# The first weighted row of each tile written by VectorE straight into the accumulator bank

## The chip, the cores and the metric

The kernel runs on one core of a Trainium2 chip. The metric is the device time of one execution in microseconds (us). All data are 32-bit floats unless said otherwise. The engines are called as in the profile: PE (TensorE, matrix multiplications into the accumulator memory PSUM), PEld (its weight loads), DVE (VectorE), ACT (ScalarE), POOL (GpSimd), SP (SyncE, which only issues transfers here).

## The reference

Four graph attention layers with residual connections on 3327 nodes of 512 features; the 3327 x 3327 adjacency is sparse (about 16 neighbours a node). Cut to what matters, with `h` the normalised input of a layer:

```python
for layer in (0, 1, 2, 3):                     # 8, 4, 1 and 8 heads
    h = relu(layernorm(x))
    v = h @ W                                  # 512 features, split into the heads
    e = leaky_relu(v . a_src[i] + v . a_dst[j], 0.2)
    alpha = softmax of e over the neighbours j of i (layers 0, 1 add the node itself)
    y[i] = sum over j of alpha[i, j] * v[j]    # per head
    x = x + (elu(y) if layer in (1, 2) else y)
```

## The kernel before

**First stage (about the first 312 us).** The adjacency is turned into lists of neighbours. The nodes are sorted by how many neighbours they have and cut into 26 tiles of 128 nodes; tile t needs at most `CAPS[t]` neighbours a node, from 36 (tile 0) down to 11 (tile 25). A list holds the node itself as well.

**The layers.** For a tile, slot k means: of each of the 128 nodes the k-th neighbour. A slot is one row of 512 features on each of 128 partitions. POOL fetches it with an indirect transfer (L834) out of a table in device memory that holds the projected features of all nodes; slot 0, the nodes themselves, comes with a plain transfer by SP from layer 1 on (L865). Slots are worked on in groups of up to four; one group is one step. (In layer 0 the first group has three, and the node itself is the last of them; in the other layers it is slot 0.) In a step `scored` (L870 to L895) makes the softmax weights: DVE adds and bends the scores (L887, L889), ACT takes the exponential into the tile `pw` in PSUM (L890). Then `group` (L897 to L921) multiplies and adds:

```python
            m = pools["m"].tile([P, GROUP, F], F32, name="m")
            for q in range(n):
                ...   # DVE: m[:, q, :] = row q of the group times the weights of its heads  (L916)
            for q in range(n):
                nc.tensor.matmul(self.po, ident, m[:, q, :], start=(k0 + q == 0), stop=(k0 + q == K - 1))
```

So DVE writes each weighted row to SBUF (the tile `m`, three buffers), and PE adds it to the tile's sum in a PSUM bank by multiplying it with the identity. `start` at slot 0 makes the first matmul overwrite the bank instead of adding to it. A 32-bit matmul is two records in the profile, each with a weight load: one slot is one DVE instruction and two matmul records. The bank is `self.po`, out of a pool with two buffers (`pools["o"]`), so that a tile's bank is used again by the tile after the next.

Layer 2 has one head and does the sum on DVE alone (L909, L911); the change does not touch it. In layers 1, 2 and 3 the 1, 9 and 2 tiles with the longest lists are not fetched by slots but worked on over all nodes ("Several" and "Wholes"; matmuls at L1298 and L1150), between the steps of the others. That leaves 26, 25 and 24 tiles in layers 0, 1 and 3 for the code above, 75 in all, with 467, 431 and 406 slots, 1304 in all.

**The order.** It is written out by hand: engines work in the order in which the program issues to them. A loop goes over the steps; transfers are issued seven groups ahead (`LOOK`). In each step come the pieces that earlier tiles put off, the `scored` of the next step, then the `group` of this one. When a tile's last group is done, its end is put off over the following steps (`ends`, L994 to L1004): two steps later DVE divides the bank by the softmax sum in place (L938), in layer 1 ACT takes it through relu and exp (L944, L946), DVE adds it to x (L958, or L954 in layer 3), ACT centres it (L966, L969), PE transposes it (L450), ACT copies it out (L457), PE multiplies by the next layer's weights (L468, 16 records into `pv`), ACT copies that out (L475) and SP writes it to the next layer's table. All of this passes through the same in-order engines as the slots do.

"Several" has sums of its own. It already begins its banks with a matmul of zeros by the identity and adds to them with `start=False` (L1290).

At the start of a layer its PSUM pools are opened anew. Layers 0 to 2 share the buffer of the projection, `pv`; before layer 3 it is given back.

## Time and profile before

| | |
|---|---|
| median of 5 runs | 2992.99 us (2977.85 to 2998.97) |
| the profiled execution | 2981.57 us, span 2979.8 us |
| PE busy | 2240.4 us (75%) |
| PE on the matmuls of L921 | 1330.4 us, 2608 records |
| DVE busy | 1912.5 us (64%) |
| DVE on the products of L916 | 811.5 us, 1304 instructions |
| ACT busy | 913.1 us (31%) |
| POOL busy | 1748.8 us (59%) |
| mean granted TensorE clock | 0.873 |

In the trace layer 0 lies at about 316 to 1130 us of the span, layer 1 up to 1864, layer 2 up to 2310 and layer 3 up to the end.

In a group of instructions (the page's list, or its answer by lines) stand the line, the engine, the operation, what it writes and reads, the shapes and the count; behind the bar the busy time, the mean duration of one in ns, the idle time of the engine just before them, and what ended most of it. "DVE m L916" is the product that wrote m; "issue" is a start for which no wait is seen; "remote" is a releaser that the profile can't name. Durations of neighbouring matmuls overlap, so the step from one start to the next says more than the duration.

### The profile page before, as it was taken

Reading aid. Unit: us, or ns where it says so; the run is one execution under the profiler, and the core shown is the slowest. Engines: PE = TensorE matmul, PEld = TensorE weight load, DVE = VectorE, ACT = ScalarE, POOL = GpSimd, SP = SyncE. Lnnn points to the kernel's source line nnn. Section 1 sums busy time; section 2 is a strip of 40 time slices with the busy share of each in tenths; the row PEclk is TensorE's granted clock in tenths of the full one; section 3 lists DMA queues with packets and bytes.
Section 4 is the critical chain, followed back from the end, with each engine's and each line's share of the span. In section 5 each row is a group of like instructions: output and inputs, shape, how many; then the busy total and the mean of one; then the engine's idle time right before and its main releaser. Section 6 shows DMA issues by size and latency. Waiting matters only on the chain.

```text
span 2979.8 us, 26822 instructions
## 1 busy us (share of the span) xinstructions
PE 2240.4 (75%) x6832; PEld 1226.9 (41%) x6832; DVE 1912.5 (64%) x5004; ACT 913.1 (31%) x2506; POOL 1748.8 (59%) x1739
## 2 busy tenths in 40 slices
PE   4777687886877655778878867688796678888787
PEld 2564243443433322444434434345354334444343
DVE  7987666654555434666656555698987456665566
ACT  5872122322221112323232222344333222322221
POOL 7985465664556636545555552676664655565654
PEclk9978898988888887989988888899898788898988
DMA  6885576776776657756666653787784666666664
GB/s 231 324 286 162 165 242 198 229 244 184 214 211 195 191 146 210 203 168 181 197 196 186 187 172 112 228 256 236 227 262 122 200 195 194 192 199 195 200 182 127
DMA packets 262490, 599.55 MB, mean 201 GB/s; under 512 B 103923, under 2 KB 121331, under 8 KB 257974
## 3 DMA queue, kind: packets, MB, share of 16 engines
q0 software_dynamic: 126128, 438.08, 50.1%
q1 hardware_dynamic: 132454, 152.86, 16.1%
q10 hardware_dynamic: 3744, 6.82, 0.7%
q8 instruction: 55, 0.90, 0.1%
q14 instruction: 109, 0.89, 0.1%
HBM read 547.96 MB, written 49.65 MB: 201 GB/s over the span
## 4 chain that ended last, share of the span: by engine, by line
PE 27%; DVE 17%; issue 13%; another core or an unknown queue 7%; ACT 4%; POOL 3%; DMA 2%; DVEq 0%; POOLq 0%; ACTq 0%; SPq 0%
PE bank L921 19%; DVE m L916 6%; PE pv L468 4%; DVE bank L911 3%; POOL g L834 3%; PE whole L1298 2%; PE whole L1150 1%; DMA g<-tab,idxb 1%; DVE z L887 1%; DVE x L958 1%; DVE z L889 1%; DVE em L1123 1%; DMA g<-tab,idxa 1%; DVE low L952 1%
## 5 line engine op out<-in xcount | busy, mean ns | idle before, releaser
L921 PE MATMUL bank<-m,ident 128*128 128x512 f32 x2608 | 1330.4, 658 | 360.0 <-DVE m L916 221.9
L916 DVE TENSOR_TENSOR m<-g,pw 128x512 f32<-128x512 f32 x1304 | 811.5, 682 | 526.9 <-ACT pw L890 252.0
L834 POOL DMA_INDIRECT g<-tab,idxb x734 | 698.2, 951 | 476.0 <-issue 200.5
L921 PEld LDWEIGHTS bank<-m,ident 128*128 128x128 f32 x2608 | 529.1, 211 | 1021.5 <-issue 636.4
L468 PE MATMUL pv<-w,hT 128*128 128x264 f32 x1664 | 433.1, 414 | 72.3 <-ACT hT L457 46.0
L834 POOL DMA_INDIRECT g<-tabx,twiceb x342 | 323.9, 947 | 242.1 <-issue 126.9
L834 POOL DMA_INDIRECT g<-tab,idxa x297 | 283.0, 953 | 248.4 <-issue 90.8
L468 PEld LDWEIGHTS pv<-w,hT 128*128 128x128 f32 x1664 | 332.8, 204 | 173.4 <-ACT hT L457 52.2
L890 ACT ACTIVATE pw<-z 128x32 f32<-128x32 f32 (+4 forms) x362 | 69.1, 191 | 817.6 <-DVE z L889 432.0
L1150 PE MATMUL whole<-ve,em 128*128 128x512 f32 x468 | 229.0, 641 | 53.7 <-DVE em L1123 15.2
L694 POOL TENSOR_TENSOR key<-a,keys 128x3328 int32<-128x3328 int32 (+1 forms) x29 | 189.3, 6531 | 16.4 <-DVE cand L703 13.0
L911 DVE SCALAR_TENSOR_TENSOR bank<-g,L,bank 128x512 f32<-128x512 f32 x243 | 183.3, 754 | 11.0 <-DVE bank L911 2.4
L1150 PEld LDWEIGHTS whole<-ve,em 128*128 128x128 f32 x468 | 93.8, 206 | 166.4 <-issue 112.6
L834 POOL DMA_INDIRECT g<-tabx,twicea x99 | 94.4, 954 | 97.7 <-issue 52.9
L475 ACT ACTIVATE v<-pv,rstd 128x528 f32<-128x528 f32 x78 | 54.1, 694 | 307.1 <-remote 134.9
L703 DVE MAX8 cand<-key 128x8 f32<-128x208 int32 x416 | 147.2, 374 | 0.1
L450 PE MATMUL pt<-ident,xn 128*128 128x128 f32 x416 | 70.5, 297 | 99.2 <-ACT xn L966 57.4
L1275 ACT ACTIVATE spare<-room,low 128x64 f32<-128x64 f32 x208 | 58.0, 336 | 192.7 <-PE bank L921 74.1
L450 PEld LDWEIGHTS pt<-ident,xn 128*128 128x128 f32 x416 | 54.6, 152 | 140.3 <-ACT xn L966 66.0
L889 DVE SCALAR_TENSOR_TENSOR z<-z 128x32 f32<-128x32 f32 (+5 forms) x434 | 83.0, 191 | 32.0 <-remote 10.7
L887 DVE TENSOR_TENSOR z<-g,pw 128x32 f32<-128x32 f32 (+4 forms) x362 | 63.3, 175 | 62.1 <-DMA g<-tab,idxa 36.7
L1264 ACT ACTIVATE r<-low,spare 128x256 f32<-128x256 f32 x208 | 98.9, 476 | 8.9 <-remote 2.1
(180 smaller groups left out, 2185.9 us busy)
## 6 DMA issues: line engine op xcount, KB each, us to landing
a<-in_adj SPq DMA_DIRECT2D x25, 1664.0 KB
tab<-v SPq DMA_DIRECT2D x78, 264.0 KB
ve<-tab SPq DMA_DIRECT2D x78, 264.0 KB
g<-tab SPq DMA_DIRECT2D x66, 264.0 KB
tabx<-vx SPq DMA_DIRECT2D x26, 528.0 KB
g<-tab,idxb POOLq DMA_INDIRECT x734
low<-tab SPq DMA_DIRECT2D x52, 132.0 KB
room<-tab SPq DMA_DIRECT2D x52, 132.0 KB
```

What stands on the lines that cost most here:

```text
L450: nc.tensor.transpose(pt[:, k, :], xn[:, k * P:(k + 1) * P], ident)
L468: nc.tensor.matmul(pv[:, s, :HF + 8], hT[:, k, :], W.w[:, k, s, :], start=(k == 0), stop=(k == KC - 1))
L694: nc.gpsimd.tensor_tensor(key[:, c:c + quarter], a[:, c:c + quarter], keys[:, c:c + quarter], OP.mult)
L703: nc.vector.max(cand[:, g * 8:(g + 1) * 8], key[:, g * SEG:(g + 1) * SEG])
L834: nc.gpsimd.indirect_dma_start(out=out_, out_offset=None, in_=table, in_offset=bass.IndirectOffsetOnAxis(ap=which, axis=0))
L887: nc.vector.tensor_tensor(z, g[:, :n, ROW - 8:ROW - 8 + H], self.s.unsqueeze(1).to_broadcast([P, n, H]), OP.add)
L889: nc.vector.scalar_tensor_tensor(z, z, SLOPE, z, OP.mult, OP.max)
L911: nc.vector.scalar_tensor_tensor(acc, v, w, acc, OP.mult, OP.add)
L916: nc.vector.tensor_tensor(m[:, q, :].rearrange("p (s h d) -> p s h d", s=2, d=D), v.rearrange("p s (h d) -> p s h d", d=D), wt[:, k0 + q, ...
L921: nc.tensor.matmul(self.po, ident, m[:, q, :], start=(k0 + q == 0), stop=(k0 + q == K - 1))
L1150: nc.tensor.matmul(tl.po.rearrange("p (s m) -> p s m", s=2), e[:, q * P:(q + 1) * P], v.rearrange("p (s m) -> p s m", s=2)[:, :, :F // 2], ...
L1264: nc.scalar.activation(self.r[:, h, :], self.a[:, g, :], AF.Relu, bias=-1.0, scale=self.b[:, j, g:g + 1])
```

## The change

The first slot of a tile (k0 + q == 0) is no longer written to `m` and added by PE: DVE writes the product into the bank itself. PE adds the other slots, none of them with `start`. So that these add to what DVE wrote, each of the two banks gets one matmul of zeros by the identity with `start=True` at the start of layers 0, 1 and 3, before the layer's first piece of work.

```diff
             m = pools["m"].tile([P, GROUP, F], F32, name="m")
             for q in range(n):
                 v = g[:, q, :].rearrange("p (s m) -> p s m", s=2)[:, :, :F // 2]
-                nc.vector.tensor_tensor(m[:, q, :].rearrange("p (s h d) -> p s h d", s=2, d=D),
+
+                out_ = self.po if k0 + q == 0 else m[:, q, :]
+                nc.vector.tensor_tensor(out_.rearrange("p (s h d) -> p s h d", s=2, d=D),
                                         v.rearrange("p s (h d) -> p s h d", d=D),
                                         wt[:, k0 + q, :H].rearrange("p (s h) -> p s h", s=2)
                                         .unsqueeze(3).to_broadcast([P, 2, H // 2, D]), OP.mult)
-            for q in range(n):
-                nc.tensor.matmul(self.po, ident, m[:, q, :], start=(k0 + q == 0), stop=(k0 + q == K - 1))
+            for q in range(k0 == 0, n):
+                nc.tensor.matmul(self.po, ident, m[:, q, :], start=False, stop=(k0 + q == K - 1),
+                                 skip_group_check=True)
...
+            if not whole:
+
+                for _ in range(2):
+                    nc.tensor.matmul(pools["o"].tile([P, BANK], F32, name="bank"), ident,
+                                     zero.to_broadcast([P, BANK]), start=True, stop=True)
```

`whole` is true in layer 2 alone.

## The prediction

> **What bounds the kernel now.** I read the shares of busy time first, then the chain of waits, then the groups, and last the order of time around the starts of tiles. From the page: busy time, the chain's shares by engine and by line, and the two groups that matter:

> ```profile
> PE 2240.4 (75%) x6832; PEld 1226.9 (41%) x6832; DVE 1912.5 (64%) x5004; ACT 913.1 (31%) x2506; POOL 1748.8 (59%) x1739
> ...
> PE 27%; DVE 17%; issue 13%; another core or an unknown queue 7%; ACT 4%; POOL 3%; DMA 2%; DVEq 0%; POOLq 0%; ACTq 0%; SPq 0%
> PE bank L921 19%; DVE m L916 6%; PE pv L468 4%; DVE bank L911 3%; POOL g L834 3%; PE whole L1298 2%; PE whole L1150 1%; DMA g<-tab,idxb 1%; DVE z L887 1%; DVE x L958 1%; DVE z L889 1%; DVE em L1123 1%; DMA g<-tab,idxa 1%; DVE low L952 1%
> ...
> L921 PE MATMUL bank<-m,ident 128*128 128x512 f32 x2608 | 1330.4, 658 | 360.0 <-DVE m L916 221.9 <-issue 134.0 <-DVE L L1280 1.8
> L916 DVE TENSOR_TENSOR m<-g,pw 128x512 f32<-128x512 f32 x1304 | 811.5, 682 | 526.9 <-ACT pw L890 252.0 <-remote 117.2 <-issue 79.4
> ```

> No engine is full. PE is the busiest and leads the chain; but the adding matmuls also stood idle 360 us, most of it until a product of DVE was there, and the products stood idle until ACT had the weights. PE, ACT and DVE pass work round in a ring, and each is late in turn. By stages (columns PE, PEld, DVE, ACT, POOL, clock, transfers), layers 0, 1, 2, 3:

> ```profile
> 316.00:1130.00 814.00, 600.90 (x1696) 301.71 (x1696) 456.67 (x1210) 179.05 (x475) 463.78 (x490) 0.86 0.69 205
> 1130.00:1864.00 734.00, 563.39 (x1602) 299.83 (x1603) 446.90 (x1202) 202.60 (x616) 383.73 (x406) 0.88 0.63 180
> 1864.00:2310.00 446.00, 346.83 (x1033) 196.45 (x1031) 363.56 (x725) 168.93 (x404) 281.62 (x298) 0.89 0.73 221
> 2310.00:2980.00 670.00, 524.91 (x1668) 278.40 (x1668) 398.66 (x837) 181.45 (x634) 387.45 (x408) 0.86 0.64 187
> ```

> In the three layers that the change touches PE is busy 74 to 78%, DVE 56 to 61%, and the clock is granted at 0.86 to 0.88.

> The chain is followed back only to 732.6 us. In the 2247 us from there, L921 holds 18.9% of the span, 563 us. L921 was busy 1077 us in the same stretch. So about 52% of the time of these matmuls lies on the path that sets the end.

> Two starts of tiles in order of time. The first is in layer 1 (its first slot is the start of the x8 at 1219.79), DVE then PE:

> ```profile
> 1219.04 2.48 DVE L916 TENSOR_TENSOR m<-g,pw 128x512 f32<-128x512 f32 x4 [0.25 <-issue]
> ...
> 1219.79 3.70 PE L921 MATMUL bank<-m,ident 128*128 128x512 f32 x8 [1.18 <-issue]
> ```

> PE was waiting: it begins 0.05 us after the first product's end. Four products take 2.48 us, so 0.62 us from one to the next. The second is in layer 3: the products begin at 2786.65, PE is still on the tile before, in an unbroken run of 14 records, and takes the new tile's first slot at 2789.31, 1.97 us after its product was done.

> ```profile
> 2784.55 8.36 PE L921 MATMUL bank<-m,ident 128*128 128x512 f32 x14 [1.04 <-issue]
> ...
> 2786.65 2.48 DVE L916 TENSOR_TENSOR m<-g,pw 128x512 f32<-128x512 f32 x4 [0.33 <-issue]
> ```

> **The change, part by part.**

> *PE's 75 first slots go* (26, 25 and 24 tiles; 150 of the 2608 records). A slot at full clock is two steps of 0.429 us, 0.86 us; at half clock 1.71 us; the mean over all is 1330.4/1304 = 1.02 us. The 1304 products and the 2608 records can be matched in order of time. For 30 of the 75 tiles PE stood waiting (0.05 to 0.10 us after the product's end); for the other 45 it was behind, by up to 5.25 us. Where it was behind it saves the whole slot. Where it was waiting it must now wait for the second product, 0.62 us more, and saves only the rest: 0.24 us warm, about 1.09 us at half clock. Each tile's own slot time, less what of the 0.62 us its lag did not cover, sums to 24 + 21 + 20 = 65 us. With 52% on the path: **-34 us**.

> *Six matmuls of zeros come* (two each in layers 0, 1, 3). 0.86 us each at full clock, 1.71 at half: 5 to 10 us. They are issued before the layer's first work, where PE waits for gathers: it stood idle 5.06, 10.31 and 10.41 us before the first slots of the three layers. In layer 0 they need the zeros (written at 312.6) and the first product starts at 315.54, so two cold ones (3.4 us) just fit. In layer 3 the new bank may be the one the projection gave back; the zeros then wait for ACT's last copy of `pv` (to 2307.4) and push back the 32 small matmuls at L1238, which begin at 2306.43. That is up to 4.4 us on a chain through ACT that ends at 2313.7 and is not needed before 2317.96, when the first gather lands. Taken: 0. Without that cover: +10 us.

> *The product's target moves from SBUF to PSUM, 75 times.* No row of before is this instruction. Below: the shortest product, 0.627 us; above: the longest DVE write to a bank, 0.757 us (L911). Against the mean 0.682 that is -4 to +6 us of DVE. Nearest is L938, the same operation on the same shape written to the same bank: 0.694. Taken: 75 x 0.012 = **+1 us**. If writes to PSUM also lose the 0.06 us by which neighbouring products overlap, 5 us more.

> *The new waits.* DVE's first product now needs the bank free, where PE's first matmul did. The bank's last reader is DVE's own L958 or L954, issued at least a step earlier in the same queue, so it waits for nothing new; behind it stand the other products, and PE behind those. In group 0 the first buffer row of `m` is unused, so DVE waits a product later for PE to free `m` (21.8 us of such waits in all): no loss. POOL's and SP's queues are not moved past; POOL gets gather buffers free when DVE is done with them, which hardly moves.

> *The clock.* PE's granted clock is 1 or 0.5 and changes every 3.4 us. One drop in layer 0 (columns as above):

> ```profile
> 601.10:604.50 3.40, 2.08 (x5) 0.57 (x3) 0.00 (x0) 0.00 (x0) 2.49 (x4) 1.00 1.01 380
> 604.50:607.90 3.40, 0.00 (x0) 0.00 (x0) 0.00 (x0) 0.00 (x0) 1.32 (x2) 1.00 0.96 358
> 607.90:611.30 3.40, 0.24 (x1) 0.24 (x2) 0.98 (x2) 0.91 (x3) 0.00 (x0) 0.50 0.18 71
> 611.30:614.70 3.40, 3.40 (x5) 1.33 (x6) 3.27 (x9) 0.00 (x0) 0.94 (x1) 0.50 0.13 52
> 614.70:618.10 3.40, 3.40 (x9) 1.50 (x8) 3.00 (x9) 1.71 (x5) 2.70 (x3) 1.00 0.61 167
> ```

> An empty stretch is followed by half clock, a full one by full clock. Over the whole trace there are 96 drops. Nearly all follow a stretch with PE busy under 0.48, and full clock comes back after one with 0.83 or more. Half clock holds for 760 us, in which PE is busy 470 us; half of those are lost, 2.45 us a drop. About 9% of the warm stretches lie between 0.43 and 0.67 busy, where 0.86 us less work can tip them: 75 x 0.09, seven more drops, 17 us of PE, 52% of it on the path: **+9 us**; from none to 20 drops, 0 to +25.

> [...]

> *What is late next.* -34 + 1 + 9 = -24. When PE is earlier, other waits end last: weights from ACT (252 us before products), the projection's way through ACT, gathers. Only rows far off bound how much stays: none (all becomes idle time of PE, as the 360 us are) or all. PE leads the chain but does not fill it, so I take 0.7: **-17 us**.

> The profiled execution took 2981.57 us (span 2979.8 and 1.8 around it); the sum gives 2965 for it. The median of the runs shown is 11 us higher, and the prediction is made for that: 2993 - 17, about **2976 us**. Its own range is 2955 to 2988.

> **The rivals.**

> *The time saved only lengthens PE's waits.* For: 30 of 75 tiles begin with PE waiting, and DVE's products themselves wait for ACT. Against: 45 begin with PE behind, and L921 leads the chain. It leaves some 5 us: 2988.

> *Slower: the clock.* One mechanism, at tile starts: PE, with a slot less and a start 0.62 us later, finds its window too empty and stays at or falls to half clock. A drop costs 2.45 x 0.52 = 1.27 us of the path. Against (34 - 1) x 0.7 = 23 us of gain, 18 more drops cancel it. If every second tile start costs one (37), it is 47 - 33 = +14: 3007. For: 15 of the 75 first slots already took 1.7 us or more, half clock's step. Against: where PE is behind its window is full anyway.

> *PE is the bound nearly throughout.* More than the 52% is on the path and nothing is lost to other waits: 35 to 65 us come off, at the far end 2928. Against: 360 us of idle time before these very matmuls.

> *The change doesn't add up right.* The matmuls without `start` must add to what DVE wrote; that a bank once begun keeps adding is what the sums of L1290 rely on only for PE's own writes. It would show in the sums, not in the time.

> **How the numbers follow.** Chances: the forecast 0.43, saved time only waits 0.22, the clock 0.21, PE throughout 0.14. 0.5% is 15 us, about what a measurement of this kernel can tell from none. Faster: the forecast's own range reaches from 5 to 38 us of gain, and some two thirds of its chance lies beyond 15 (0.28); with PE throughout, 0.42. Within: the rest of the forecast and nearly all of the first rival, 0.35. Slower: the clock, and a little of the unknown costs (10 us of zeros, 10 us of writes), 0.23. The range takes part of the full 65 us at the low end, and at the high one the clock with the uncovered zeros: 2938 to 3014.

> **What would show it.** The adding matmuls at 2458 records and about 77 us less busy; twelve records of zeros at the layer starts; 75 products into `bank` near 0.69 us; PE's starts at new tiles up to 0.62 us later where it waited. Clock: 0.87 kept and under 105 drops, or the clock rival holds. The prediction is wrong if idle time before L921 grows by as much as its busy time falls, or if the 75 writes take over 0.8 us.

## The result, and the profile after

| | before | after |
|---|---|---|
| median | 2986.93 us (94 runs, 2961.25 to 3015.14) | 2984.04 us (52 runs, 2957.09 to 3012.87) |
| the profiled execution | 2981.57 us, span 2979.8 | 2979.67 us, span 2977.9 |
| PE busy | 2240.4 us | 2201.1 us |
| PE on the adding matmuls (L921, now L923) | 1330.4 us, 2608 records | 1269.7 us, 2458 records |
| idle time before them | 360.0 us | 387.5 us |
| DVE on the products (L916, now L918) | 811.5 us | 766.2 + 52.2 = 818.4 us |
| idle time before them | 526.9 us | 398.9 + 131.1 = 530.0 us |
| mean granted TensorE clock | 0.873 | 0.862 |

The ratio after to before is 0.9983, with a 95% interval of 0.997 to 0.9997: about 5 us are gained (1 to 9; the two medians differ by 2.9), well within the 0.5% that the prediction counted as no change. The forecast was a gain of 17 us. The two groups of products overlap, so their sum of 818.4 us overstates them: DVE as a whole is busy 1913.8 us after and 1912.5 before.

The page of the changed kernel: busy time, the chain's shares by engine and by line, the adding matmuls, the products into `m`, and the products into the bank.

```profile
PE 2201.1 (74%) x6694; PEld 1211.5 (41%) x6694; DVE 1913.8 (64%) x5004; ACT 913.8 (31%) x2506; POOL 1748.8 (59%) x1739
...
PE 18%; DVE 17%; issue 12%; another core or an unknown queue 9%; ACT 5%; POOL 5%; DMA 2%; SPq 1%; DVEq 0%; POOLq 0%; ACTq 0%
PE bank L923 12%; DVE m L918 6%; POOL g L834 4%; PE pv L468 3%; DVE bank L911 3%; PE whole L1301 1%; PE whole L1153 1%; ACT r L1267 1%; DVE z L889 1%; DVE z L887 1%; DVE x L961 1%; DMA g<-tab,idxb 1%; ACT spare L1278 1%; DVE low L955 1%
...
L923 PE MATMUL bank<-m,ident 128*128 128x512 f32 x2458 | 1269.7, 664 | 387.5 <-DVE m L918 244.6
L918 DVE TENSOR_TENSOR m<-g,pw 128x512 f32<-128x512 f32 x1229 | 766.2, 682 | 398.9 <-ACT pw L890 211.0
...
L918 DVE TENSOR_TENSOR bank<-g,pw 128x512 f32<-128x512 f32 x75 | 52.2, 696 | 131.1 <-ACT pw L890 90.3
```

The 150 records of PE are gone, and the adding matmuls are down from 19% to 12% of the chain. But PE as a whole is busy 39.3 us less and idle 37.4 us more (span less busy: 739.4 us before, 776.8 after). What left PE's busy time came back as PE's waiting. The last two rows show the engine ahead of PE: DVE's products still stand idle 530 us (527 before), 301 us of it until ACT has the weights (252 before). The work ahead of PE in a step waits as long as it did.

The stages, with the columns of the prediction (PE, PEld, DVE, ACT, POOL, clock, share and rate of transfers), layers 0, 1, 2 and 3:

```profile
316.00:1130.00 814.00, 597.61 (x1680) 303.02 (x1680) 464.40 (x1230) 182.81 (x489) 475.95 (x503) 0.86 0.71 210
1130.00:1864.00 734.00, 546.12 (x1538) 290.24 (x1539) 445.03 (x1193) 202.36 (x612) 378.29 (x400) 0.86 0.62 179
1864.00:2310.00 446.00, 345.29 (x1012) 196.93 (x1011) 355.40 (x708) 165.32 (x392) 274.42 (x291) 0.87 0.71 215
2310.00:2980.00 670.00, 503.82 (x1626) 269.39 (x1624) 399.01 (x837) 182.15 (x634) 386.80 (x407) 0.85 0.65 187
```

In layers 1 and 3, whose stretches hold nearly the same work as before, PE's busy share falls from 77 and 78% to 74 and 75%, and the clock from 0.88 and 0.86 to 0.86 and 0.85. From the first product to the last, layer 0 takes 769.8 us (783.2 before), layer 1 706.3 (697.9) and layer 3 643.7 (642.2). In this one pair of executions the layers move by more than the change is worth as a whole, and in both directions.

### The profile page after: what moved, and what is told of

Read it like the earlier page. It is cut to its first block, busy times and chain, and to the rows that moved or that the text cites. A ratio compares the mean times of both kernels' runs of the same rounds, so it can differ in the third digit from the quotient of the medians.

```text
span 2977.9 us, 26484 instructions
## 1 busy us (share of the span) xinstructions
PE 2201.1 (74%) x6694; PEld 1211.5 (41%) x6694; DVE 1913.8 (64%) x5004; ACT 913.8 (31%) x2506; POOL 1748.8 (59%) x1739
## 4 chain that ended last, share of the span: by engine, by line
PE 18%; DVE 17%; issue 12%; another core or an unknown queue 9%; ACT 5%; POOL 5%; DMA 2%; SPq 1%; DVEq 0%; POOLq 0%; ACTq 0%
PE bank L923 12%; DVE m L918 6%; POOL g L834 4%; PE pv L468 3%; DVE bank L911 3%; PE whole L1301 1%; PE whole L1153 1%; ACT r L1267 1%; DVE z L889 1%; DVE z L887 1%; DVE x L961 1%; DMA g<-tab,idxb 1%; ACT spare L1278 1%; DVE low L955 1%
## 5 line engine op out<-in xcount | busy, mean ns | idle before, releaser
L923 PE MATMUL bank<-m,ident 128*128 128x512 f32 x2458 | 1269.7, 664 | 387.5 <-DVE m L918 244.6
L918 DVE TENSOR_TENSOR m<-g,pw 128x512 f32<-128x512 f32 x1229 | 766.2, 682 | 398.9 <-ACT pw L890 211.0
L834 POOL DMA_INDIRECT g<-tab,idxb x734 | 698.4, 951 | 483.7 <-issue 205.6
L923 PEld LDWEIGHTS bank<-m,ident 128*128 128x128 f32 x2458 | 500.5, 212 | 1015.0 <-issue 594.5
L468 PE MATMUL pv<-w,hT 128*128 128x264 f32 x1664 | 439.7, 419 | 81.8 <-ACT hT L457 52.6
L834 POOL DMA_INDIRECT g<-tabx,twiceb x342 | 324.4, 948 | 231.7 <-issue 133.6
L834 POOL DMA_INDIRECT g<-tab,idxa x297 | 282.6, 951 | 238.5 <-issue 93.2
L468 PEld LDWEIGHTS pv<-w,hT 128*128 128x128 f32 x1664 | 337.7, 207 | 186.9 <-ACT hT L457 59.7
L890 ACT ACTIVATE pw<-z 128x32 f32<-128x32 f32 (+4 forms) x362 | 69.2, 191 | 826.3 <-DVE z L889 461.3
L911 DVE SCALAR_TENSOR_TENSOR bank<-g,L,bank 128x512 f32<-128x512 f32 x243 | 183.3, 754 | 11.0 <-remote 2.0
L834 POOL DMA_INDIRECT g<-tabx,twicea x99 | 94.4, 954 | 96.7 <-issue 54.0
L918 DVE TENSOR_TENSOR bank<-g,pw 128x512 f32<-128x512 f32 x75 | 52.2, 696 | 131.1 <-ACT pw L890 90.3
L887 DVE TENSOR_TENSOR z<-g,pw 128x32 f32<-128x32 f32 (+4 forms) x362 | 63.4, 175 | 72.7 <-DMA g<-tab,idxa 36.6
```

What stands on the lines that cost most here:

```text
L468: nc.tensor.matmul(pv[:, s, :HF + 8], hT[:, k, :], W.w[:, k, s, :], start=(k == 0), stop=(k == KC - 1))
L834: nc.gpsimd.indirect_dma_start(out=out_, out_offset=None, in_=table, in_offset=bass.IndirectOffsetOnAxis(ap=which, axis=0))
L887: nc.vector.tensor_tensor(z, g[:, :n, ROW - 8:ROW - 8 + H], self.s.unsqueeze(1).to_broadcast([P, n, H]), OP.add)
L911: nc.vector.scalar_tensor_tensor(acc, v, w, acc, OP.mult, OP.add)
L918: nc.vector.tensor_tensor(out_.rearrange("p (s h d) -> p s h d", s=2, d=D), v.rearrange("p s (h d) -> p s h d", d=D), wt[:, k0 + q, :H].re ...
L923: nc.tensor.matmul(self.po, ident, m[:, q, :], start=False, stop=(k0 + q == K - 1), skip_group_check=True)
```

## The experiments

The open question was where the 34 us went that the prediction laid on the path. Four readings stood against one another, and the expectations call them by letters. Theory A: PE's freed time is mostly off the path, and part of it turns into half clock. Theory B: it is worth about what the prediction took, and a new cost gave most of it back. Then, after the first four runs: POOL's gathers set the pace and hide PE's slots (Theory C), or the ring through DVE does (Theory D).

The runs were made on four chips, and the kernel before takes a different time on each: 2460.74, 2459.66, 3029.90 and 2456.88 us. The figures of 2987 us in the expectations are those of the main comparison. Every ratio below is against the kernel before on the same chip. What differs between the chips has a part of its own below.

### The zeros alone

The kernel before, with only the six matmuls of zeros:

```diff
                     pw = pools["p"].tile([P, BANK], F32, name="pw")
+            if not whole:
+                for _ in range(2):
+                    nc.tensor.matmul(pools["o"].tile([P, BANK], F32, name="bank"), ident,
+                                     zero.to_broadcast([P, BANK]), start=True, stop=True)
```

> The kernel before, with only the six matmuls of zeros added at the starts of layers 0, 1 and 3. Theory A (the freed PE time is mostly off the path, and part of it goes to a colder clock): 2987, as before, within 4 us. Theory B (the freed time is worth its 15 to 25 us, and a new cost gives most of it back), if that cost is the zeros: 5 to 10 us slower than before.

Measured: 2460.05 us against 2460.74, ratio 0.9995 (0.9984 to 1.0006). On this chip the zeros cost nothing that can be measured.

### The change with PE's work put back

After the change, a matmul of zeros is added to each tile's first group, so that DVE writes to the bank as in the change but PE has as many slots as before:

```diff
+            if k0 == 0:
+                nc.tensor.matmul(self.po, ident, zero.to_broadcast([P, BANK]), start=False, stop=False,
+                                 skip_group_check=True)
             for q in range(k0 == 0, n):
```

> The changed kernel, but PE adds a matmul of zeros to the bank in the place of each of the 75 slots it no longer adds. PE has the work of before again; the write by DVE into the bank and the zeros at the layer starts stay. Theory A: within 5 us of before, on the slower side by the second product that PE now waits for at tile starts (about 30 tiles x 0.62 us, half of it on the path: up to +9). Theory B, if the write or its waits are the cost: 12 to 20 us slower than before.

Measured: 2461.63 us, 1.0002 (0.9991 to 1.0014). Nor do the 75 writes to PSUM, here. But the next runs show that this chip hides hundreds of us of PE's work, so it can hide a small cost too: the two runs speak against Theory B on this chip only. Where the kernel takes 2987 us, only the trace speaks on the two costs (in the part on the prediction).

### One more slot of each tile taken off PE

Here the second slot is left out of each tile's sum:

```diff
-            for q in range(k0 == 0, n):
+            for q in range(2 * (k0 == 0), n):
```

> The changed kernel, in which PE also leaves out the second slot of each tile (75 more slots; DVE still makes the product, so the sums lack that neighbour). Nothing is added for it, so this is the price of 75 PE slots alone. Theory A: 2 to 10 us less than the changed kernel, and a clock lower by some 0.005 to 0.01. Theory B: 15 to 25 us less than the changed kernel.

Measured: 2463.24 us, 1.0013 (1.0002 to 1.0025), with a clock of 0.933 (before 0.948). PE is busy 1999.3 us, 88 less than in the run with the zeros alone, and the time is, if anything, 3 us longer. Neither Theory A's 2 to 10 us less nor Theory B's 15 to 25 came about.

### Every other slot taken off PE

Every other slot but the last is left out of the sums, 599 of 1229:

```diff
             for q in range(k0 == 0, n):
+                if (k0 + q) % 2 and k0 + q < K - 1:
+                    continue
```

> The changed kernel, in which PE leaves out every slot of odd number but the last of a tile: nearly half of all slots, some 580 (their neighbours are missing from the sums; DVE still makes all products). About 500 us of PE work at full clock. Theory A: 40 to 100 us less than the changed kernel, less than a fifth of what is taken off, and a clock under 0.82. Theory B, with half of PE's time on the path: 180 us less or more.

Measured: 2461.22 us, 1.001 (0.9998 to 1.0022), clock 0.857. Its page, busy time and the adding matmuls:

```profile
PE 1740.8 (71%) x5496; PEld 975.4 (40%) x5496; DVE 1919.3 (78%) x5004; ACT 910.7 (37%) x2506; POOL 1749.2 (71%) x1739
...
L925 PE MATMUL bank<-m,ident 128*128 128x512 f32 x1260 | 799.0, 747 | 457.7 <-DVE m L918 445.6
```

The same two lines with the zeros alone, on the same chip:

```profile
PE 2087.4 (85%) x6844; PEld 1166.4 (47%) x6844; DVE 1919.9 (78%) x5004; ACT 911.2 (37%) x2506; POOL 1750.7 (71%) x1739
...
L921 PE MATMUL bank<-m,ident 128*128 128x512 f32 x2608 | 1199.6, 606 | 128.9 <-DVE m L916 128.3
```

PE does 347 us less work, its matmuls stand idle 329 us longer before DVE's products, and the kernel takes as long. On this chip PE's slots are worth nothing, and even Theory A's 40 to 100 us less did not come. The clock does fall, from 0.948 to 0.857, but so low a clock with so much less work cost no time here, so half clock is no reason for the missing gain on this chip. The chain of waits of the run with the zeros alone had given L921 10% of the span, some 250 of its 1200 us, a fifth; taking away a third of those 1200 us moved nothing.

### Which engine sets the pace: the change beside four edits

On the next chip the change itself ran beside edits that relieve one engine each.

> The changed kernel itself, beside before on the chip of these runs. Theory C (POOL's gathers set the pace, one every 1.25 us, and PE's slots are hidden behind them whatever the chain of waits says): within 0.15% of before where before takes about 2461 us; where it takes about 2987 us, 0 to 0.3% less. Theory D (the ring through DVE sets the pace): the same, since DVE keeps its number of products.

The change: 2462.16 us against 2459.66, 1.0007 (0.9995 to 1.002); clock 0.941 against 0.947. On this chip the change gains nothing, as both readings have it. Busy time:

```profile
PE 2042.0 (83%) x6694; PEld 1144.1 (47%) x6694; DVE 1917.3 (78%) x5004; ACT 909.9 (37%) x2506; POOL 1748.6 (71%) x1739
```

**Fewer gathers.** Slot 1 is filled by a plain transfer of SP with the tile's own rows, so the sums are over other rows. That takes 92 gathers off POOL (1739 instructions become 1647), the 17 tiles of layer 2 among them:

```diff
-                if l > 0 and k0 + q == 0:
+                if k0 + q == 1:
+                    table = tabs[l % 2] if l > 0 else tabx[:, :ROW]
+                    nc.sync.dma_start(g[:, 1, :], table[t * P:(t + 1) * P, :])
+                elif l > 0 and k0 + q == 0:
```

> The changed kernel, in which the second slot of each tile is filled by a plain transfer that SP issues, not by a gather of POOL (these rows are then those of the wrong nodes). DVE, ACT and PE do the same work; POOL issues 75 gathers fewer, 75 x 1.25 = 94 us. Theory C: 50 to 95 us less than the changed kernel where before takes about 2461 us. Theory D: under 15 us less.

Measured: 2392.30 us, 0.9729 (0.9712 to 0.9746), 70 us less than the change on the same chip: Theory C's 50 to 95, not Theory D's under 15. Both runs move 599.5 MB, so it is not the volume of the transfers. Busy time:

```profile
PE 2023.3 (85%) x6694; PEld 1136.9 (48%) x6694; DVE 1906.9 (80%) x5004; ACT 909.8 (38%) x2506; POOL 1662.4 (69%) x1647
```

**Fewer products.** DVE leaves out the product of slot 1, and PE adds that of slot 2 twice, so PE's work stays:

```diff
             for q in range(n):
+                if k0 + q == 1:
+                    continue
...
-                nc.tensor.matmul(self.po, ident, m[:, q, :], start=False, stop=(k0 + q == K - 1),
+                nc.tensor.matmul(self.po, ident, m[:, q + (k0 + q == 1), :], start=False, stop=(k0 + q == K - 1),
```

> The changed kernel, in which DVE leaves out the product of the second slot of each tile and PE adds the third slot twice in its place. DVE loses 75 x 0.62 = 46 us, all else stays. Theory C: within 6 us of the changed kernel. Theory D: 20 to 46 us less.

Measured: 2450.81 us, 0.997 (0.9955 to 0.9986). DVE's products into `m` take 721.3 us instead of 766.1, 45 us less; the time is 11 us less than the change's, a quarter. That is more than Theory C's 6 us and less than Theory D's 20 to 46: the products count a little.

**Nearly no slots on PE.** Only the last slot of each tile is added to the sum; 1154 of 1229 are left out:

```diff
             for q in range(k0 == 0, n):
+                if k0 + q < K - 1:
+                    continue
```

> The changed kernel, in which PE adds only the last slot of each tile; DVE makes all products, the sums lack the others. 1154 of the 1229 slots go, about 990 us of PE at full clock. Theory C, where before takes about 2461 us: within 8 us of before, as with every other slot left out. Where before takes about 2987 us: if PE's slots were worth anything there, as the chain of waits with its 19% says, 200 us less or more; if not, under 60 us less.

Measured: 2451.64 us, 0.9971 (0.9959 to 0.9983), clock 0.723. PE is busy 1248.4 us instead of 2042.0, 794 us less, for 10.5 us of time: 1% of it. Busy time:

```profile
PE 1248.4 (51%) x4386; PEld 853.6 (35%) x4386; DVE 1918.8 (78%) x5004; ACT 908.8 (37%) x2506; POOL 1748.9 (72%) x1739
```

So on this chip the gathers of POOL set the pace, and not PE. POOL's timeline of the change shows how (start, duration, engine, line, and in brackets the idle time before):

```profile
399.63 0.95 POOL L834 DMA_INDIRECT g<-tabx,twicea  x1 [0.30 <-issue]
400.88 0.95 POOL L834 DMA_INDIRECT g<-tabx,twicea  x1 [0.30 <-issue]
402.13 0.94 POOL L834 DMA_INDIRECT low<-in_adj,idxb  x1 [0.30 <-issue]
403.38 0.94 POOL L834 DMA_INDIRECT g<-tabx,twicea  x1 [0.31 <-issue]
```

One gather begins every 1.25 us: 0.95 us busy and 0.30 us of issue, without a wait. Of the 1533 gathers in the layers, 98% begin so, within 0.32 us of the end of POOL's instruction before. A window over all layers of the same run (PE, PEld, DVE, ACT, POOL):

```profile
312.00:2460.00 2148.00, 1834.68 (x5852) 991.02 (x5850) 1663.06 (x3960) 728.40 (x2123) 1513.47 (x1598) 0.95 0.80 243
```

POOL's 1513.47 us look like 70% and PE's 1834.68 like 85%. But POOL's steps of at most 0.31 us from one instruction to the next sum to 468 us, so POOL is taken for 1513 + 468 = 1981 of 2148 us, 92%. The 92 gathers less are 92 x 1.25 = 115 us of it, and 70 us came off. The gathers that went were replaced by plain transfers, so some of the 70 could be due to rows that land earlier; that wasn't separated.

### The same questions on a chip where the kernel before takes 3030 us

In the main comparison the kernel before takes 2987 us, and its waits differ from those of the two chips so far, so the question had to be put again. The next three runs were made where it takes 3029.90 us, with waits of the same kind as in the main comparison. In that, POOL is not taken so fully: beyond steps of 0.31 us it stands idle 683 us in the layers before the change, and 163 us in the run of the change above. First, PE was given more work, a matmul of zeros at the start of each group but a tile's first (287 slots of 0.86 us, 247 us):

```diff
             for q in range(n):
+                if k0 > 0 and q == 0:
+                    nc.tensor.matmul(self.po, ident, zero.to_broadcast([P, BANK]), start=False, stop=False)
                 nc.tensor.matmul(self.po, ident, m[:, q, :], start=(k0 + q == 0), stop=(k0 + q == K - 1))
```

> The kernel before, with one matmul of zeros more at the start of every group but a tile's first: 287 slots, 287 x 0.86 = 247 us of PE added, nothing else changed. Theory C (POOL's gathers set the pace and PE has slack): under 25 us slower than before where before takes about 2461 us, a tenth of what is added. If PE's share of the chain (23% in the run with the zeros only) were worth its time: 55 us slower or more.

Measured: 3052.04 us, 1.0066 (1.0046 to 1.0087), 22 us more, where the share of the chain asked for 55 or more. Its chain by engine and the adding matmuls:

```profile
PE 38%; DVE 14%; issue 12%; another core or an unknown queue 6%; ACT 4%; DMA 2%; POOL 2%; DVEq 0%; POOLq 0%; ACTq 0%; SPq 0%
...
L923 PE MATMUL bank<-m,ident 128*128 128x512 f32 x2608 | 1282.5, 633 | 228.1 <-DVE m L916 127.8
```

PE holds 38% of the chain now, and still only 9% of the work that it was given shows in the time. The clock rose from 0.868 to 0.898, and an adding matmul took 633 ns (658 in the profile before): part of the added work was paid for by warmer matmuls. The change took 65 us of slots off PE by the prediction's working, and 5 us came off the time: 8%. So PE's time came out worth as little with work added as with work taken off. But the added matmuls need no product, so they can fall into PE's waits: the adding matmuls stand idle 228.1 us here, and 360.0 in the profile before, on another chip. Leaving out many slots, the stronger test, was not run where the kernel takes 2987 or 3030 us.

Then both kernels with POOL relieved. All odd slots were filled by SP's plain transfers with the tile's own rows (sums over other rows again), once in the kernel before and once in the changed one; POOL's 1739 instructions become 984:

```diff
-                if l > 0 and k0 + q == 0:
+                if (k0 + q) % 2:
+                    table = tabs[l % 2] if l > 0 else tabx[:, :ROW]
+                    nc.sync.dma_start(g[:, q, :], table[t * P:(t + 1) * P, :])
+                elif l > 0 and k0 + q == 0:
```

> The kernel before with the odd slots filled by plain transfers of SP in place of POOL's gathers (wrong rows, same bytes; some 620 gathers fewer, about 775 us of POOL). POOL no longer sets the pace; PE and DVE are left. Theory C: 150 to 300 us less than before.

> The changed kernel with the odd slots filled in the same way (wrong rows). Against the run of before with the same rows this shows what the change is worth once gathers are cheap. Theory C, with PE as the next bound: 25 to 60 us less than that run. If DVE or transfers are the next bound: within 8 us of it.

Measured: 2374.36 us without the change (0.7835, 0.782 to 0.7851) and 2361.55 us with it (0.7792, 0.7775 to 0.7809). The first is 655 us less than the kernel before, over twice the 150 to 300 expected, and below the 2460 us of the faster chips: the gathers hold the kernel up here too, by more than was understood (755 x 1.25 = 944 us of POOL went). Here too plain transfers took their place. The five runs of the one (2374.22 to 2375.99) and of the other (2352.68 to 2365.01) do not overlap: the change is worth 12.8 us, 0.54%, where most gathers are out of the way. That lies between the two expectations (25 to 60 us with PE as the next bound, within 8 without). Busy time and the adding matmuls without the change:

```profile
PE 2063.4 (87%) x6832; PEld 1165.5 (49%) x6832; DVE 1909.9 (80%) x5004; ACT 913.5 (39%) x2506; POOL 1036.4 (44%) x984
...
L924 PE MATMUL bank<-m,ident 128*128 128x512 f32 x2608 | 1187.2, 604 | 80.2 <-DVE m L919 65.5
```

and with it:

```profile
PE 2010.4 (86%) x6694; PEld 1134.2 (48%) x6694; DVE 1909.5 (81%) x5004; ACT 908.3 (39%) x2506; POOL 1035.9 (44%) x984
...
L926 PE MATMUL bank<-m,ident 128*128 128x512 f32 x2458 | 1131.8, 607 | 98.8 <-DVE m L921 69.7
```

Here PE does lead: without the change it holds 19% of the chain against DVE's 6%, is busy 87%, and its adding matmuls stand idle only 80 us. Even so, of the 53 us that PE is busy less, 19 us return as idle time before the same matmuls, and a quarter of the 53 shows in the time.

### A version that beats both

If gathers set the pace, a tile that is taken out of the gathering should pay. In layer 3 a third tile is worked on over all nodes instead of by slots, on top of the change:

```diff
-DENSE = [0, 1, 9, 2]
+DENSE = [0, 1, 9, 3]
```

> The changed kernel with three tiles of layer 3 worked on over all nodes instead of two (the list of their numbers a layer is 0, 1, 9, 3). 22 gathers of POOL fewer (27 us at 1.25), 23 slots fewer for PE and DVE; in their place 416 more matmul records at L1301 (some 60 us of PE) and larger steps for ACT and DVE. Theory C (gathers set the pace, PE has slack): 10 to 27 us less than before, on either kind of chip. If PE or DVE bounds layer 3: 10 to 40 us more.

Measured: 2429.53 us against 2456.88, 0.988 (0.9859 to 0.99): 27 us, 1.2%, the upper end of what Theory C gave. POOL issues 1717 instructions instead of 1739, and 22 x 1.25 = 27.5 us. That the two numbers are equal fits the reading and does not prove it, since the edit also moves work between PE and DVE. Whether the change has any part in this gain wasn't separated; the run of the change alone, on another chip, gained nothing.

## Why the prediction was right or wrong

The time fell inside the range, and on the side of "within 0.5%", to which 0.35 was given. The forecast of 2976 us was not the case that came about: by the ratio 5 of its 17 us came. That the median still lies only 8 us from it is in part luck, since the kernel before came out at 2987 us and not at the 2993 from which the forecast starts.

*PE's 75 first slots go.* Right in count (2608 to 2458 records), and 75 slots of 1.02 us left. But the 1229 that stayed got slower, 1.033 us each (1269.7/1229), which is 16 us: 61 us less busy and not 77. At new tiles PE begins one product later, as worked out: at the start of layer 3 the first product began at 2322.73 and PE at 2323.47 before (0.74 us); after, 2321.11 and 2322.45 (1.34 us).

*With 52% on the path, -34 us.* This is the step that failed, and the factor of 0.7 behind it did not make up for it. The share of the chain was read as the worth of the time. The chain says which of several events came last, not by how much; in a ring of engines the next one can be close behind, and here it was. Where the share was put to the test it didn't hold: about 8% came off here, 9% went on where PE got more to do, 0% where a third of the slots' time was taken away (a fifth of it was on the chain there), and some 20% (12.8 of 65 us) with most gathers out of the way. 52% was seen nowhere. What does set the pace where the kernel takes 2987 us is not shown; on the chip with 2460 us it is the gathers.

*Six matmuls of zeros.* Right at 0, on both counts. In layer 0 the four records took 3.29 us, from 309.69 to 312.98; the second product, the first that PE adds, was done about 0.1 us later, and PE took it at 313.22. In layer 3 the bank that the projection gave back was indeed awaited. The timeline of PE there:

```profile
2299.03 6.04 PE L468 MATMUL pv<-w,hT 128*128 128x264 f32 x16 [0.69 <-ACT hT L457]
2305.91 1.99 PE L1381 MATMUL bank<-zero,ident 128*128 128x512 f32 x4 [0.84 <-ACT v L475]
2307.74 1.05 PE L1241 MATMUL r<-ident,low 128*128 128x128 f32 x8
```

The zeros wait 0.84 us for ACT's copy of `pv`, and the small matmuls behind them begin at 2307.74. The last of them ends at 2314.33 and ACT's copy behind it at 2314.96. The scores that open the layer's work on DVE wait for the first gathered rows until 2315.84:

```profile
2315.84 0.19 DVE L887 TENSOR_TENSOR z<-g,pw 128x32 f32<-128x32 f32 x1 [17.57 <-DMA g<-tab,idxa]
```

ACT stands idle until their exponential at 2316.29. So the push is hidden, by the cover that was named, with 1.3 us to spare.

*The product into PSUM.* Right: 0.696 us beside 0.682 (taken: 0.694), and DVE as a whole is busy 1.3 us more, so the overlap of neighbours, 5 us in the prediction's aside, was not lost. *The new waits.* Right: of the 131.1 us before the products into the bank, 90.3 ended with ACT's weights, and none is put down to the bank.

*The clock.* About the forecast size. Counted in stretches of 3.4 us, the drops went from 96 to 101 (forecast: seven more), and half clock held for 827 us instead of 760, with PE busy in 506 us of it instead of 470: 18 us of PE lost, where 17 were forecast. This is one pair of executions, and the mean clock of the changed kernel lies anywhere from 0.859 to 0.871 over its runs. But on the chip of the four edits the median clock fell from 0.947 to 0.941 with the change, and on the chip of the first four runs, with PE's work put back, it stayed (0.949 after 0.948). Only 20 of the 96 drops and 21 of the 101 followed an empty stretch. These counts and clocks stand with the rows of the trace from which the term was worked out. But the prediction priced a drop at 52% of PE's loss, and this falls with the step above: where 599 slots were left out, the clock fell to 0.857 at no cost in time.

*What is late next.* The factor of 0.7 was far too mild: what is late next is late almost at once. It was named rightly in the text (weights from ACT, gathers), and the rows for it were there: the products' idle time of 527 us, and the wait for ACT's weights in it (252 us before; 211.0 + 90.3 after).

*The rivals.* "The time saved only lengthens PE's waits" is what happened, with its forecast of some 5 us. The evidence given against it (45 of 75 tiles begin with PE behind, L921 leads the chain) didn't weigh what it was taken to weigh: that PE is behind at a tile's start says nothing on whether it is still behind when the next thing waits for it. "The clock" as a loss did not come about, nor "PE throughout". (The clock rival's +14 for 37 drops sets 47 us against the full gain of 33; against the 23 us of the sentence before it, it would have been +24.) That the sums would not add up did not come about either: in the changed kernel PE's 2458 records without `start` added to what DVE's 75 products had written in the banks.

*The sign of being wrong.* The prediction was to be wrong if the idle time before L921 grew by as much as its busy time fell. It grew by 27.5 us and the busy time fell by 60.7, so the sign did not show, though the gain stayed away. It looked at one line: over PE as a whole, 39.3 us less of work stand against 37.4 more of waiting.

## What to carry to other kernels

A share of the chain of waits tells where to look, and not what time is worth there: take a piece of work away, or add some, and see what part of it shows in the time. The busy share can leave out issuing, as it did here with the 0.30 us of each of POOL's gathers; count instructions and take the step from one start to the next (POOL looked 70% busy and was taken for 92%). When the engine that leads the chain gets less to do, look first at the idle time of the engines ahead of it: if that stays, as the products' 527 and 530 us did here, do not count on the gain.

## What was not expected of the hardware

**One gather took POOL 1.25 us**, 0.95 busy and 0.30 of issue, from one start to the next in the run of the change where the kernel before takes 2459.66 us (starts at 399.63, 400.88, 402.13 and 403.38 us). By the runs above the gathers pace the kernel where the kernel before takes 2460 us.

**The same program takes 2457 to 3030 us, depending on the chip, though the work of DVE and POOL takes as long.** A product takes 682 ns in the profile before (2981.57 us) and 683 ns in that with the zeros alone (2467.48 us), a gather 951 and 953 ns. One thing that differs in the traces is the time from the end of one engine's work to the start of the next engine's on it. In the profile before, layer 0, PE:

```profile
595.83 3.06 PE L468 MATMUL pv<-w,hT 128*128 128x264 f32 x13
598.72 4.45 PE L921 MATMUL bank<-m,ident 128*128 128x512 f32 x10
```

and ACT, which copies `pv` out, in the same execution:

```profile
609.50 0.70 ACT L475 ACTIVATE v<-pv,rstd 128x528 f32<-128x528 f32 x1 [13.32 <-remote]
```

The last of the matmuls into `pv` ended at 598.9 us and ACT was free, but the copy began at 609.50. The last raise of PE's count before it is recorded at 609.47. Take as a delay the time from the end of the matmuls, or of ACT's instruction before if that is later, to the start of the copy. Over the 78 copies the delays sum to 209.5 us in the profile before (22 of over 2 us, the longest 24.8) and to 166.1 after, but to under 2 us in the runs with the zeros alone and with the change where the kernel before takes 2460 us. With 755 gathers fewer they sank to 26.0 us, on a chip where giving PE more work had left them at 168.5. So on that chip they fell where gathers went and plain transfers took their place. The traces differ in their records as well: 5.7 landings a transfer are recorded in the profile before, 15.97 with the zeros alone. Whether the recording has a part in the delays, why only some chips show them, and what they share with the gathers stays open; no run here tells it. The chain of waits has 6 to 9% of "another core or an unknown queue" in the three profiles with such delays (before, after, PE given more work), and none with the zeros alone. What part of the 500 us between the chips it makes is also open: the delays of this one copy are only the part that can be read off plainly.
